# Ten routed groups in one part, scattered in three batches beside the edge lists, with pairs ordered by node tile

## The chip, the cores and the metric

The kernel runs on one core of one Trainium2 chip. The metric is the device time of one execution in microseconds (us). The kernel before took 2046.94, 2055.24 and 2054.68 us in three runs, a median of 2054.68 us. The profiled execution took 2045.04 us, of which 2043.3 us are the span of the trace.

Engines are named as the profile does: PE (matrix multiplications), PEld (its weight loads), ACT (ScalarE), DVE (VectorE), POOL (GpSimd) and SP (SyncE, which here only issues DMAs).

## The reference, cut to what matters

There are 128 graphs of 64 nodes, which make 8192 rows of 256 features. Two layers follow each other; each is a graph step and a feed-forward step, both added to x. The change lies in the feed-forward step of layer 1, except for one piece of memory that it fills in layer 0. That step is:

```python
h = (x_flat @ W_gat).reshape(M, HEADS, NUM_EXPERTS)
e = leaky_relu(a_src[src] + a_dst[dst])         # for every edge, and a loop at every node
alpha = softmax of e over the edges that end in the same node
agg = segment_sum(h[src] * alpha, dst) + b_gat
scores = layernorm(agg).reshape(M, HEADS, NUM_EXPERTS).mean(1)
topk_s, topk_i = top_k(scores, 2)               # 2 of 4 experts for every node
w = softmax(topk_s)
for ei in range(4):
    g = where(topk_i == ei, w, 0).sum(-1)
    out = out + g * (gelu(x @ W1[ei] + b1[ei]) @ W2[ei] + b2[ei])
```

The edges decide by which two experts a node is computed. Until a node's edges are summed, nobody knows which two these are.

## The kernel before

The 8192 rows are 64 node tiles of 128 rows, or 16 groups of 4 tiles. x stays in on-chip memory throughout.

**Layer 0.** Parts of two groups run one after another: a graph step (`graph`), and two parts behind it the first half of the feed-forward step (`gated`), which writes 4 KB rows to the DRAM buffer `hrows`, sorted by expert, with indirect DMAs from POOL (line 775). A row tile is turned by copies of ACT (line 713) into one buffer, `rows`, which must have landed in DRAM before the next group's copies. Beside them DVE looks through chunks of the edge list (`collect`): each chunk is loaded by SP (`src` and `dst`, line 247), searched, and what is left over is stored by SP (`left`, line 284), after which the next chunk uses the same buffer. `hrows` gets zeros at its experts' starts (line 815), from a 128 x 128 tile of zeros.

**Layer 1, two ways to apply the experts.** Groups 0 to 7 (`DENSE`) are computed densely: all four experts for every row (`experts`, `dense`). A unit of this work is one step of the generator `units`: eight for an expert (four of the first matmul with its Gelu, four of the second), 32 for a group, 256 in all. Their results are kept in DRAM (`ystore`) until the gates are known (`kept`, `add`). Groups 8 to 15 are routed: every row is sent only to the buffers of its two experts.

The routed groups come in two parts of 16 tiles. For each part `gates` computes ranks and weights, `route` gives each row its place, `send` copies a row tile twice and scatters it to `zslots` (two indirect DMAs a tile, line 1904), `pairs` takes two tiles of slots at a time through one expert, whose number is read into registers, and stores the result in `yslots`, and `back` gathers two results for every row (line 2100), copies them, and adds them with their weights. Slots of one expert are rounded up to whole pairs of tiles, so a part has RT + 3 = 19 pairs, 38 in all.

**Order of the work in layer 1.** The tables of the graph attention come first; 72 units of dense work lie beside them. A short prologue takes 20 units. Then `edges_of_lists` works through 16 sorted edge lists, one for each group, routed groups first. It has 162 steps; in each of the first 144 POOL gathers 128 edge sources (`got`, line 1585), a copy moves them on three steps later, and a list is summed into `acc` 8 steps behind its last gather. Two of three steps also take a dense unit. From list 6 on each step takes one step of the gates and routes; in the last 18 steps it takes one scatter. The rest of part 0's scatters follow, with units and the gates of the dense groups, then the 38 pairs with part 1's scatters, part 0's gathers and the kept results beside them, then the last 40 units with part 1's gathers beside them.

The order within an engine is drawn up when the program is built: what is ready first goes out, by its place in the text where several are ready. `tc.issue_after(ins)` puts what its block issues on the engine of `ins` behind `ins`. SP and POOL each take their DMAs strictly in order; a DMA that has to wait holds up those behind it.

Of the kernel before, what the change touches and what calls it, by code (L numbers as in the profile page):

```python
# [2 lines left out]

# [64 lines left out]
PARTS = 2  # L68
ROUTED = 4 * PARTS
DENSE = NG - ROUTED  # L70
RT = ROUTED // PARTS * GR
PAIRS = RT + 3
# [8 lines left out]
def kernel(  # L81
# [103 lines left out]
    yrows = dram.tile([NSLOT * P, D], F32, name="yrows")  # L185
    psel = const.tile([P, NT], F32, name="psel")
# [233 lines left out]
    with tc.tile_pool(name="w0", bufs=1, reuse_waits="tile") as w0, tc.tile_pool(name="kp", bufs=1, reuse_waits="tile") as kp:  # L420
# [29 lines left out]
        with tc.tile_pool(name="bg1", bufs=1, reuse_waits="tile") as bg1, tc.tile_pool(  # L450
# [19 lines left out]
            with tc.tile_pool(name="b2", bufs=1, reuse_waits="tile") as b2, tc.tile_pool(  # L470
# [321 lines left out]
                chunks = iter(range(n_chunks))  # L792
                for i in range(n_parts + 2):
# [18 lines left out]
                    if i == 1:  # L812
                        with tc.issue_after(first_made[-1]):
                            for e in range(E0):
                                nc.sync.dma_start(
                                    hrows[e * N : e * N + P, :].rearrange("p (k f) -> p k f", f=P),
                                    none.unsqueeze(1).to_broadcast([P, FD // P, P]),
                                )
# [261 lines left out]
    zns = dram.tile([ROUTED, P, GR * D], F32, name="zns")  # L1080
    zslots = [dram.tile([PAIRS * 2 * P, D], F32, name=f"zslots{h}") for h in range(PARTS)]
    yslots = [dram.tile([PAIRS * 2 * P, D], F32, name=f"yslots{h}") for h in range(PARTS)]
# [485 lines left out]
    def edges_of_lists(pool, psum, td3):  # L1568
# [5 lines left out]
        for step in range(ET * (NB + 2)):  # L1574
            n, at = divmod(step, ET)
            if n < NB:
                b = lists[n]
                if at == 0:
                    fss[n] = pool.tile([P, ET, CH], F32, name="fs")
                    sorting = sort(lists[n + 2], pool, psum) if n + 2 < NB else iter(())  # L1580
                    el = pool.tile([P, ET * P], BF16, name="el")
# [7 lines left out]
                if at == 3:  # L1589
                    to = pool.tile([P, ET, P], BF16, name="to")  # L1590
# [153 lines left out]

    place = [gp.tile([P, 2, RT], I32, name=f"place{h}") for h in range(PARTS)]
    weight = [gp.tile([P, 2, RT], F32, name=f"weight{h}") for h in range(PARTS)]
    pair_e = [gp.tile([P, PAIRS], I32, name=f"pair_e{h}") for h in range(PARTS)]
    T0 = DENSE * GR
    sends = []

    def gates(pool, t0, t1, ranks):
# [3 lines left out]
        def of(name, *shape):  # L1755
            return pool.tile([P, *shape, nt], F32, name=name)
# [4 lines left out]
        def by_node(v, n):  # L1761
# [5 lines left out]
        agg = of("agg", HC)  # L1767
# [4 lines left out]
            sums[:, HEADS:CH, :].rearrange("p (h c) t -> p h c t", c=NEXP),  # L1772
# [55 lines left out]
    def route(h, pool, ranks, psum):  # L1828

        t0 = T0 + h * RT  # L1830
        rk, gt = ranks[t0], gate[:, :, t0 : t0 + RT]
        chosen = pool.tile([P, NEXP, RT], BF16, name="chosen")
        V.tensor_scalar(chosen, rk, 1.5, None, ALU.is_lt)
        flat = chosen.rearrange("p e t -> p (e t)")

        pt = psum()
        nc.tensor.matmul(pt[0 : NEXP * RT, 0:P], flat, ones, start=True, stop=True)
        tots = pool.tile([NEXP * RT, P], BF16, name="tots")
        V.tensor_copy(tots, pt[0 : NEXP * RT, 0:P])
        yield  # L1840
        pr = psum()
        nc.tensor.matmul(pr[:, 0 : NEXP * RT], before, flat, start=True, stop=False)
        nc.tensor.matmul(pr[:, 0 : NEXP * RT], tots, later[:, 0 : NEXP * RT], start=False, stop=True)
        row = pool.tile([P, NEXP, RT], F32, name="row")
        V.tensor_copy(row.rearrange("p e t -> p (e t)"), pr[:, 0 : NEXP * RT])
        pa = psum()
        nc.tensor.matmul(pa[:, 0:NEXP], tots, of_all, start=True, stop=True)
        yield
        full = pool.tile([P, NEXP], I32, name="full")
        V.tensor_scalar(full, pa[:, 0:NEXP], float(2 * P - 1), None, ALU.add)  # L1850
        V.tensor_scalar(full, full, 8, None, ALU.logical_shift_right)
        end = pool.tile([P, NEXP + 1], F32, name="end")
        V.memset(end[:, 0:1], 0.0)
        V.tensor_copy(end[:, 1:], full)
        for e in range(1, NEXP):
# [335 lines left out]
```

## Time and profile before

| | us |
|---|---|
| median of three runs | 2054.68 |
| profiled execution | 2045.04 |
| span of its trace | 2043.3 |
| PE busy | 1877.0 (92%) |
| DVE busy | 1339.2 (66%) |
| ACT busy | 948.5 (46%) |
| POOL busy | 431.2 (21%) |
| first of the 139 gathers that follow the first five | 1392.9 |
| last gather of the edge lists | 1627.8 |
| first matmul of the pairs | 1690.2 |
| first matmul behind the pairs | 1970.7 |
| last matmul | 2039.6 |

The times in the lower half are starts, counted from the start of the span, except the last matmul's, which is its end. Busy times are means over stages with different limits: a stage must be read by itself. An engine's row names what it waited for last. "issue" is time in which it waited for nothing that the trace shows.

### The profile page before, as it was taken

The page shows a single profiled execution, that of the slowest core. Times are in us where ns is not written, and L with a number is a line of the kernel's source. Part 1 is how long each engine was busy: PE and PEld are TensorE (multiplying, and loading weights), DVE is VectorE, ACT ScalarE, POOL GpSimd, SP SyncE. Part 2 cuts the span into 40 slices and gives each one's busy share as a digit, 9 for nine tenths or more (in the row PEclk, how much of TensorE's full clock was granted, in tenths as well). Part 3 has the DMA queues.
Part 4 walks back from the last instruction along what each step waited for, and adds up shares of the span by engine and source line. Part 5 has one row for each costly group of instructions (what it writes and reads, how often), then busy time and mean ns, then how long its engine had stood idle before and what let it go on. Part 6 is the DMA issues. An engine that isn't in the chain of part 4 may idle for free. (4 is left out here: it accounts for less than half of the span.)

```text
span 2043.3 us, 32233 instructions
## 1 busy us (share of the span) xinstructions
PE 1877.0 (92%) x10582; PEld 1329.1 (65%) x10582; DVE 1339.2 (66%) x4364; ACT 948.5 (46%) x1740; POOL 431.2 (21%) x464
## 2 busy tenths in 40 slices
PE   7889989899996999999487999998899999999999
PEld 5444444444455999998354766666666757888876
DVE  6789988861218888887598775857678552334435
ACT  4867677666662222222267677432233333333332
POOL 2011011010110000000442100015566652303223
PEclk9999999989997999999798999999999999999999
DMA  9232223242424444545215211373222248978843
GB/s 296 64 103 102 95 76 127 75 135 69 165 83 165 159 163 151 161 152 154 75 56 157 75 50 54 125 223 77 58 47 66 62 160 275 300 240 279 281 130 98
DMA packets 223037, 274.93 MB, mean 135 GB/s; under 512 B 55696, under 2 KB 175888, under 8 KB 222864
## 3 DMA queue, kind: packets, MB, share of 16 engines
q1 hardware_dynamic: 188976, 212.26, 33.3%
q0 software_dynamic: 23040, 60.22, 9.1%
q8 instruction: 90, 1.47, 0.3%
q10 hardware_dynamic: 10848, 0.30, 0.3%
q14 instruction: 83, 0.68, 0.1%
HBM read 159.40 MB, written 113.22 MB: 133 GB/s over the span
## 5 line engine op out<-in xcount | busy, mean ns | idle before, releaser
L462 PE MATMUL ph<-zT,w 128*128 128x512 f32 x512 | 247.7, 608 | 5.7 <-ACT zT L704 4.7
L973 PE MATMUL py<-wd,hTt 128*128 x1088 | 247.0, 380 | 0.0
L973 PEld LDWEIGHTS py<-wd,hTt 128*128 128x128 f32 x1088 | 202.4, 191 | 24.9
L958 ACT COPY hTt<-th 128x512 f32<-128x512 f32 x136 | 73.2, 589 | 283.3 <-PE th L955 265.9
L1585 POOL DMA_INDIRECT got<-tsrc,esrc x144 | 151.8, 1054 | 179.2 <-DVE esrc L1556 75.6
L1116 PE MATMUL py<-w,hT 128*128 128x256 f32 x736 | 173.6, 388 | 8.0 <-DVE kt L1524 4.6
L1106 PE MATMUL ph<-zT,w 128*128 128x512 f32 x368 | 171.3, 608 | 0.0
L1185 POOL DMA_INDIRECT yin<-yrows,row_y x64 | 65.3, 1021 | 476.4 <-SPq L1029 360.2
L462 PEld LDWEIGHTS ph<-zT,w 128*128 128x128 f32 x512 | 93.2, 194 | 105.4 <-issue 86.2
L1116 PEld LDWEIGHTS py<-w,hT 128*128 128x128 f32 x736 | 138.3, 193 | 34.8 <-issue 10.8
L2070 ACT ACTIVATE hT<-ph,b1e 128x256 f32<-128x256 f32 x152 | 72.1, 474 | 176.2 <-PE ph L2066 100.8
L2066 PE MATMUL ph<-zTp,w1e 128*128 128x256 f32 x608 | 139.0, 382 | 4.3 <-DMA w1e<-in_L_ffn_W_dram 4.3
L1110 ACT ACTIVATE hT<-ph,b 128x512 f32<-128x512 f32 x92 | 63.1, 688 | 163.6 <-PE ph L1106 137.6
L2079 PE MATMUL py<-w,hT 128*128 x608 | 137.5, 379 | 0.0
L2087 DVE TENSOR_TENSOR y<-py,b2e 128x256 f32<-128x256 f32 x76 | 32.2, 424 | 159.8 <-PE py L2079 147.3
L775 POOL DMA_INDIRECT hrows<-rows,pos x64 | 63.5, 992 | 335.3 <-issue 212.5
L2066 PEld LDWEIGHTS ph<-zTp,w1e 128*128 128x128 f32 x608 | 116.5, 192 | 20.6 <-issue 4.5
L624 PE MATMUL pre<-wd 128*128 128x512 f32 x256 | 125.2, 606 | 1.9 <-ACT wd L610 1.3
L465 ACT ACTIVATE hT<-ph,b 128x512 f32<-128x512 f32 x128 | 88.0, 688 | 74.1 <-PE ph L462 71.3
L2079 PEld LDWEIGHTS py<-w,hT 128*128 128x128 f32 x608 | 112.6, 190 | 13.8
L199 DVE TENSOR_TENSOR one<-iota_l,pb 128x2048 bf16<-128x2048 bf16 x96 | 116.7, 1216 | 0.1
L1106 PEld LDWEIGHTS ph<-zT,w 128*128 128x128 f32 x368 | 68.3, 193 | 68.8 <-issue 68.0
(427 smaller groups left out, 3714.6 us busy)
## 6 DMA issues: line engine op xcount, KB each, us to landing
hin<-hrows SPq DMA_DIRECT2D x68, 512.0 KB
w1e<-in_L_ffn_W_dram SPq DMA_DIRECT2D x38, 512.0 KB
yin<-ystore SPq DMA_DIRECT2D x24, 512.0 KB
zslots<-none SPq DMA_DIRECT2D x38, 256.0 KB
zin<-zslots SPq DMA_DIRECT2D x38, 256.0 KB
yslots<-y SPq DMA_DIRECT2D x76, 128.0 KB
ystore<-y SPq DMA_DIRECT2D x72, 128.0 KB
bd<-in_L_ffn_bd_dram SPq DMA_DIRECT2D x68, 128.0 KB
```

What stands on the lines that cost most here:

```text
L199: V.tensor_tensor(o, numbers.unsqueeze(1).to_broadcast(shape), of.rearrange("p (j e) -> p j e", e=2).unsqueeze(2).to_broadcast(shape), ALU ...
L462: nc.tensor.matmul(ph, w1[:, c, q * P : q * P + P], zT[:, c, :], start=(c == 0), stop=(c == 1))
L465: gelus.append(S.activation(hT, ph, AF.Gelu, bias=b1[:, q : q + 1]).ins)
L624: nc.tensor.matmul(pre, xnT[:, c, n * P : n * P + P], wcat[:, c, :], start=(c == 0), stop=(c == 1),)
L958: S.copy(hT[:, i : i + GR, :].rearrange("p q n -> p (q n)"), th)
L973: nc.tensor.matmul(py, hT[:, q, :], wd[:, bass.ds(e, 1), q, :].rearrange("p e f -> p (e f)"), start=(q == 0), stop=(q == NH - 1),)
L1106: nc.tensor.matmul(ph, w1[:, e, c, q * P : q * P + P], zT[:, c, :], start=(c == 0), stop=(c == 1))
L1116: nc.tensor.matmul(py, hTs[q][:, k * P : k * P + P], w2[:, e, q, :], start=(q == 0), stop=(q == NH1 - 1))
L1585: nc.gpsimd.indirect_dma_start(got, None, tsrc, bass.IndirectOffsetOnAxis(ap=esrc[:, b, at : at + 1], axis=0))
L2066: nc.tensor.matmul(ph, w1e[:, c, q * P : q * P + P], zT[:, c, :], start=(c == 0), stop=(c == 1))
L2070: pace[:] = [S, S.activation(hT, ph, AF.Gelu, bias=b1e[:, q : q + 1]).ins]
L2079: nc.tensor.matmul(py, hTs[q][:, k * P : k * P + P], w2[:, e, q, :].rearrange("p e f -> p (e f)"), start=(q == 0), stop=(q == NH1 - 1),)
```

## The change

It does the following.

- Groups 6 to 15 are routed, ten for eight; the dense groups are 0 to 5. All routed groups form one part of 40 tiles, with 43 pairs.
- Each expert has a fixed stretch of `zslots` and `yslots`, long enough for all 5120 rows, so a row's place is known as soon as those before it are counted. A running count (`run`) is carried from tile to tile.
- Gates, routes and scatters come in batches of 4, 3 and 3 groups, all inside the loop over the edge lists; a batch starts when its lists are summed. The scatter reads the loaded row tile itself, without the copy.
- The pairs are put in the order of the node tiles that fill them (`order_pairs`), and their rows' addresses are read into registers. `back` takes a tile when the pairs that may hold its rows are through, so that most gathers lie beside later pairs.
- All 192 dense units lie before the pairs; the gates of the dense groups and the kept results lie beside them.
- The zeros in `zslots` and `yslots` (2 x 20,480 rows of 1 KB) are written in layer 0, as 40 DMAs of 1 MB, five in each of eight parts. They were written to `zslots` alone, 38 DMAs of 256 KB, beside the edge lists.
- Two tiles of the edge lists, `el` and `to`, have one buffer for two.

```diff
-PARTS = 2
-ROUTED = 4 * PARTS
-DENSE = NG - ROUTED
-RT = ROUTED // PARTS * GR
-PAIRS = RT + 3
+ROUTED = (4, 3, 3)
+DENSE = NG - sum(ROUTED)
+STARTS = [DENSE + sum(ROUTED[:h]) for h in range(len(ROUTED))]
+T0 = DENSE * GR
+RT = NT - T0
+CAP = RT * P
+PAIRS = RT + NEXP - 1
...
+    zslots = dram.tile([NEXP * CAP, D], F32, name="zslots")
+    yslots = dram.tile([NEXP * CAP, D], F32, name="yslots")
...
+                zeros = ((to, at) for to in (zslots, yslots) for at in range(0, NEXP * CAP, 8 * P))
                 for i in range(n_parts + 2):
...
+                    if i >= 2:
+                        with tc.issue_after(gelus[-1]) if gelus else ExitStack():
+                            for to, at in islice(zeros, -(-2 * NEXP * CAP // (8 * P * n_parts))):
+                                nc.sync.dma_start(
+                                    to[at : at + 8 * P, :].rearrange("(p r) (k f) -> p (r k) f", r=8, f=P),
+                                    none.unsqueeze(1).to_broadcast([P, 8 * D // P, P]),
                                 )
...
-                    el = pool.tile([P, ET * P], BF16, name="el")
+                    el = single.tile([P, ET * P], BF16, name="el")
...
-                    to = pool.tile([P, ET, P], BF16, name="to")
+                    to = single.tile([P, ET, P], BF16, name="to")
...
     def route(h, pool, ranks, psum):
...
+        for t in range(nt):
+            V.tensor_tensor(run[:, r0 + t + 1, :], run[:, r0 + t, :], chosen[:, :, t], ALU.add)
+            if t % 4 == 3:
+                yield
+        pr = psum()[:, 0 : NEXP * nt].rearrange("p (e t) -> p e t", e=NEXP)
+        nc.tensor.matmul(pr, before, chosen, start=True, stop=False)
+        nc.tensor.matmul(pr, ones, run[:, r0 : r0 + nt, :].rearrange("p t e -> p e t"), start=False, stop=True)
+        row = by_tile("row")
+        V.tensor_tensor(row, pr, bases.unsqueeze(2).to_broadcast([P, NEXP, nt]), ALU.add)
...
+    def order_pairs(pool, psum):
...
+        V.tensor_scalar(own, own, key, None, ALU.is_le)
+        V.tensor_reduce(key, own, AX.X, ALU.add)
+        V.scalar_tensor_tensor(key, key, float(P), own_p, ALU.mult, ALU.add)
+        keys = pool.tile([P, P], F32, name="keys")
+        V.tensor_copy(keys, key.to_broadcast([P, P]))
+        yield
+        pk = psum()[:, 0:P]
+        nc.tensor.transpose(pk, keys, ident)
...
     def send(h, pool):
...
+        for t in range(r0, r0 + 2):
+            load(t)
+        for t in range(r0, r1):
+            if t + 2 < r1:
+                load(t + 2)
             zn = zs.pop(t)
             for j in range(2):
-                z = to["y"]()
-                paced_copy(z, zn)
                 sent = nc.gpsimd.indirect_dma_start(
-                    zslots[h], bass.IndirectOffsetOnAxis(ap=place[h][:, j, t : t + 1], axis=0), z, None
+                    zslots, bass.IndirectOffsetOnAxis(ap=place[:, j, t : t + 1], axis=0), zn, None
                 )
...
-    sz = ctx.enter_context(tc.tile_pool(name="sz", bufs=2, reuse_waits="tile"))
+    sz = ctx.enter_context(tc.tile_pool(name="sz", bufs=4, reuse_waits="tile"))
...
+            for h, n in enumerate(ROUTED):
+                last = STARTS[h] + n - DENSE - 1
+                while taken < ET * (last + 2):
+                    yield
+                yield from gates(ga, STARTS[h] * GR, (STARTS[h] + n) * GR, ranks)
                 yield from route(h, ga, ranks, to["ph"])
-        steps = routes()
-        zeros = ((h, i) for h in range(PARTS) for i in range(PAIRS))
-        for taken, _ in enumerate(edges_of_lists(emp, psm, td3)):
-
-            if taken % 3 == 0:
-                for h, i in zeros:
-                    nc.sync.dma_start(
-                        zslots[h][2 * P * i : 2 * P * i + 2 * P].rearrange("(k p) f -> p k f", p=P),
-                        none.unsqueeze(1).to_broadcast([P, 2, D]),
-                    )
-                    break
-            if taken > ET * (ROUTED // PARTS + 2):
-                next(steps, None)
-
-            if taken >= ET * NB:
-                next(sending)
-            if taken % 3 != 2:
-                next(units)
...
+                ready.append(h)
+            yield from order_pairs(ga, to["ph"])
+
+        def all_sends():
+
+            for h in range(len(ROUTED)):
+                while h not in ready:
+                    yield
+                yield from send(h, sz)
+
+        routing, sending = routes(), all_sends()
+        for taken, _ in enumerate(edges_of_lists(emp, em1, psm, td3)):
+
+            next(routing, None)
+            next(routing, None)
+            next(sending, None)
+            if taken * 5 % 8 < 5:
+                g, n = next(units, (g, n))
...
-            nc.sync.dma_start(z, zslots[h][2 * P * i : 2 * P * i + 2 * P].rearrange("(k p) f -> p k f", p=P))
+            nc.sync.dma_start(z, zslots[rows, :].rearrange("(k p) f -> p k f", p=P))
...
-                nc.sync.dma_start(yslots[h][(2 * i + k) * P : (2 * i + k + 1) * P, :], y)
-                yield h
+                store = nc.sync.dma_start(yslots[rows, :].rearrange("(k p) f -> k p f", p=P)[k], y)
+                alone(store, stores + gathers)
+                stores.append(store.ins)
+                yield m if k else m - 1
...
+    def back():
+
+        later = 4
+        got = {}
         for n in range(2 * RT + later):
             if n < 2 * RT:
                 t, j = divmod(n, 2)
+                while finished < min(t + NEXP - 1, PAIRS - 1):
+                    yield
+                got[n] = backs[n % len(backs)]
+                made = nc.gpsimd.indirect_dma_start(
+                    got[n], None, yslots, bass.IndirectOffsetOnAxis(ap=place[:, j, t : t + 1], axis=0)
                 )
+                gathers.append(made.ins)
             if n >= later:
                 t, j = divmod(n - later, 2)
+                xs = x[:, T0 + t, :]
+                with tc.issue_after(sums[0]):
+                    V.scalar_tensor_tensor(
+                        xs, got.pop(n - later), weight[:, j, t : t + 1], xs, ALU.mult, ALU.add
+                    )
...
+    the_pairs = pairs()
+    next(the_pairs)
+    for g, n in units:
         pass
-    steps = back(PARTS - 1)
-    for n, _ in enumerate(units):
-        next(steps, None)
-        if n % 3 == 2:
+    last_gates, returned, stored = gates(ga, 0, T0, ranks), back(), kept()
+    for n, finished in enumerate(the_pairs):
+        for of in range(2):
+            next(last_gates, None)
+        if n % 3 != 1:
+            next(returned, None)
+        if n > 30 and n % 9 == 8:
             next(stored, None)
```

## The prediction

> **What bounds the kernel now.** I read the table of slices first (PE is at 9 nearly everywhere), then the busy time by stretches of layer 1, then the chain that ended last, POOL's groups of instructions, and last SP's timeline in layer 0, where the change adds DMAs.
>
> Stretches: the edge lists, their last sum, the last scatters, the pairs, the dense tail. Columns are length, then busy time (and count) of PE, PE's weight loads, DVE, ACT and POOL, then clock, DMA share and GB/s.
>
> ```profile
> 1392.00:1628.00 236.00, 224.61 (x1601) 155.56 (x1599) 171.27 (x668) 83.22 (x169) 145.93 (x139) 0.99 0.25 55
> 1628.00:1642.00 14.00, 14.00 (x69) 10.80 (x68) 5.76 (x20) 5.28 (x9) 9.23 (x9) 1.00 0.53 179
> 1642.00:1690.00 48.00, 38.91 (x139) 25.30 (x137) 24.62 (x78) 13.71 (x26) 24.30 (x24) 0.96 0.48 164
> 1690.00:1971.00 281.00, 280.76 (x1366) 246.89 (x1367) 99.01 (x234) 103.90 (x235) 63.51 (x64) 0.99 0.83 261
> 1971.00:2043.00 72.00, 68.58 (x240) 45.20 (x238) 34.45 (x89) 18.43 (x36) 31.56 (x32) 1.00 0.34 104
> ```
>
> PE is busy 95% of the edge stretch and all of the pairs: there, less PE work is less time, as long as nothing else takes its place. The chain around the pairs (start, length, what):
>
> ```profile
> 1678.29 4.04 DMA zslots<-y,place
> 1685.48 4.62 DMA w1e<-in_L_ffn_W_dram
> 1690.24 5.23 PE ph L2066 x16
> ...
> 1959.92 0.44 PE ph L2049 x4
> 1960.36 3.46 PE py L2079 x16
> 1963.81 3.45 PE ph L2066 x16
> ...
> 1984.49 6.87 PE ph L1106 x16
> 1991.36 6.91 PE py L1116 x32
> ```
>
> One pair is 3.45 + 0.44 + 3.46 = 7.35 us, one expert pass of a dense group 6.87 + 6.91 = 13.78 us. POOL in the edge stretch, and two gathers in a row:
>
> ```profile
> L1585 POOL DMA_INDIRECT got<-tsrc,esrc x139 | 146.7, 1055 | 102.4 <-DVE fs L1132 29.8 <-ACT fs L1132 29.3 <-issue 26.3
> L1904 POOL DMA_INDIRECT zslots<-y,place x18 | 19.2, 1064 | 8.9 <-issue 4.5 <-DVE y L1132 2.7 <-DVE y L1120 1.4
> ...
> 1441.40 0.95 POOL L1585 DMA_INDIRECT got<-tsrc,esrc  x1 [0.30 <-ACT fs L1132]
> 1442.65 0.95 POOL L1585 DMA_INDIRECT got<-tsrc,esrc  x1 [0.30 <-issue]
> ```
>
> An indirect DMA holds POOL for 0.95 us at least and is followed by 0.30 us in which nothing is waited for. So the 139 gathers need 146.7 + 139 x 0.30 = 188 us of the 236 us. POOL is hidden, but has only 48 us to spare. Last, the stretch in layer 0 where zeros are written now, and two waits that touch DMA there (total, times, longest):
>
> ```profile
> 33.87 17.25 SPq L815 DMA_DIRECT2D hrows<-none  x8
> 53.97 2.72 SPq L877 DMA_DIRECT2D yrows<-none  x4
> 77.48 0.33 SPq L247 DMA_DIRECT2D src<-in_L_ffn_edge_index_dram  x1
> ...
> 50.00:54.00 4.00, 3.14 (x14) 1.54 (x12) 0.62 (x2) 3.72 (x5) 0.00 (x0) 1.00 0.96 289
> ...
> ACT rows L713 <- DMA hrows<-rows,pos: 17.0, 10, 5.6
> DVE key L251 <- DMA left<-key: 13.7, 8, 2.2
> ```
>
> A fill with 512-byte rows runs at 289 GB/s with the DMA engines full (0.96). The zeros of line 877 go out at 54 us although they are written far behind in the program: a DMA that waits for nothing goes out when SP is free.
>
> **Matmul work.** Two dense groups fewer: 2 x 4 x 13.78 = 110.2 us less. RT grows to 40, so 43 pairs for 38: 5 x 7.35 = 36.7 us more. Net 73.5 us less on PE. Counting units (a group has 32): before, 72 lie in the graph stage, 20 beside the tables, 108 in the edge loop, 16 beside the last scatters, 40 behind the pairs. After, 72, 20 and 100, none later. So the gain comes as 68.9 us behind the pairs, 27.6 us beside the scatters, 13.8 us in the edge loop.
>
> **Edge loop.** It takes in 80 scatters where it had 18, one a step, from about step 62 (the first four lists are summed at step 44, the gates and the route take two steps of their generators a loop step) to step 141. With 100 units instead of 108 a step without a scatter loses 8/162 x 1.72 = 0.08 us of the 1.69 it takes (1392.9 to 1627.8, 139 gathers): 1.61. A step with one takes POOL 1.06 + 0.30 + 0.99 + 0.30 = 2.65 us by mean rows (0.99 is the mean of all 64 scatters), 0.95 + 0.30 + 0.96 + 0.30 = 2.51 by the shortest. PE has 224.6/139 - 0.08 = 1.54 us of work in it. So 59 x 1.61 + 80 x 2.65 = 307 us (296 at the shortest): the last gather moves from 1628 to 1700 (1689). PE draws its units forward and then idles some 60 us.
>
> What queues behind POOL's wait for the first places is the gathers; five buffers cover three steps. The row loads now stand on SP between the ystore stores; a late one stalls POOL, bounded by one landing (4.0 us) for each of three batches: 0 to 12 us. I take 0, since rows are loaded two tiles ahead.
>
> **From the last gather to the first pair.** Before, the last list's sum left PE at 1641.3, 13.5 us behind the last gather. The scatters have landed by then (4.0 us behind step 141), so the 35 us of waiting for them go. What is late next: the list's memory has to come free for the pair buffers, then registers and the weight load, 1684.8 to 1690.2 now, 5.4 us. Bounds: 11 us if these run early, 19 if one after the other. I take 15, the middle, because the trace shows no placement: first pair at 1715, for 1690.2.
>
> **Pairs and end.** 43 x 7.35 + 2 us for the first, slow one (5.23 for 3.45) = 318 us: to 2033. DMA moves 261 GB/s now without holding PE; I count 49.6 MB for the pairs, 10.5 gathered, 8.4 out, 12.6 reloaded, 81 MB in 316 us = 257 GB/s. The same, so no stall. The gathers back wait on each pair's store, but their sums are placed two tiles later, so DVE meets landed data. Behind the last pair nothing covers the way home: y 0.4, store 2.5 (issued 1971.2, the next gather ran at 1973.6), two gathers 2.2, landing 2.2, sum 0.5, out 2.4 = 10.3 us, for 3.7 now: 2043.3. Layer 1 sums to 0, bounds -18 (shortest periods, early loads) to +20 (a stall of 12, late loads).
>
> **Costed at nothing.** Gates of 24 tiles and all 24 reloads now lie beside the pairs, where DVE is busy 99 of 281 us; uncovered, the gates would add about 15 us. Route, order_pairs and the third set of gates add some 15 us to DVE in the edge loop (171 of 236 now). The copies that go (128 of 0.3 to 0.4 us) are off the path. The 38 fills that go lie at 1317 to 1365, with PE 76.7 of 78 us busy: no gain. Single el and to buffers: el is fetched six steps ahead; uncovered, 16 x 2.8 us.
>
> **The new fill in layer 0.** Both buffers now have 20,480 rows: 41.9 MB of zeros, forty 1 MB DMAs with 512-byte rows, 145 us of full DMA engines at 289 GB/s. The order wrapper names a ScalarE instruction and the fill is on SP, so I expect what line 877 shows: it goes out from about 57 us, to about 240 us with the other traffic (some 12 MB). Two things meet it. The scatters of hrows (2.1 MB, four groups in that time) now land as the next copy needs them; if they get half the engines, 2.1 MB at 289 GB/s is 7 us more each: 28 us. The chunk loop of DVE (left out, src in) waits 2 us; behind the 2 MB that SP has queued (7 us: 51 to 58 us at 289 GB/s), seven chunks lose up to 49 us. Ends: 0, all hidden, and 77. I take 20, near the lower end, because PE and DVE have 8 and 12% idle there, and DVE is only 48% and then 21% busy after 400 us, so chunks can slip.
>
> The Trainium skill (DMA: Bandwidth & Descriptors, Queues, rings and completion order) says that each DMA engine goes round its queue rows packet by packet. By that the scatters keep half the engines, the 28 us above; a queue served strictly in order of arrival would cost them only the 7 us of backlog. No row here shows the two queues full together.
>
> **Rivals.** (1) The fill lies in idle DMA time (share 0.3 at 100 to 400 us) and costs 0 for 20 us: 2050, no change. For it: SP's idle gaps. Against: the copy that already waits 5.6 us on hrows. It gets below 2044 only if layer 1 lands more than 6 us under its sum. (2) All forty fills stand in SP's queue ahead of chunk 1's load (77.5 us now): DVE stops until about 205 us, some 100 us lost: 2150. For it, line 877's place; against, SP issued eight fills of 0.5 MB in 17 us, so others can slip between. (3) The edge loop stays PE-bound and the matmul gain arrives: 73.5 less 6.6 of end, 67 us faster: 1990, faster than before. It needs POOL's 188 + 80 x 1.29 = 291 us to fit in 230: scatters of 0.5 us each decide it, and none of 64 took under 0.95. 1.0 us for a scatter with its gap would give 2047.
>
> **How the numbers follow.** 2045.0 (profiled: span 2043.3 and 1.7 around it) + 0 + 20 = 2065; the three runs lie 1.9 to 10.2 us above the profiled one, I add 5: 2070. Forecast 0.47, (1) 0.29, (2) 0.13, (3) 0.07, rest 0.04. The range, 2028 to 2130, leaves out (3), most of (2) and little else; the likeliest case's own is 2050 to 2110. Half a per cent of the median 2054.7, about what a measurement can tell, is 10 us: faster by more (below 2044) takes (3), 0.12 of (1) and 0.05 of the forecast's low end: 0.24; within it lie 0.13 of (1) and 0.07 of the forecast: 0.2; slower: 0.56.
>
> **What would show it.** Right: last gather near 1700 plus the shift of layer 0, POOL periods of 2.5 to 2.65 us where scatters run, PE idle there, first pair 15 us behind, 43 pairs of 7.35 us, 10 us of end. Fills from 57 us at a DMA share near 1, longer waits at lines 713 and 251. Wrong: hidden fills, or scatters that find POOL idle.

## The result and the profile after

The changed kernel took 2126.07, 2125.81, 2132.71 and 2142.27 us, a median of 2129.39 us; the kernel before took 2046.94, 2055.24, 2054.68 and 2049.0 us, a median of 2051.84. The ratio is 1.0391, 95% interval 1.0338 to 1.0444. The forecast was 2070: the direction was right and the size was not. The profiled execution took 2126.07 us (span 2124.3).

Its page, busy tenths in 40 slices of 53 us, shows where: PE falls from 9 to between 5 and 8 from 1487 to 1805 us, while POOL is at 5 to 7 up to 1752 and the granted PE clock at 7 or 8.

```profile
PE   7888889999988999997779999989755578999997
POOL 2011111010110000001521000036667571122222
PEclk9999999999998999998879999999877778999999
```

The stretches of layer 1 after: gathers alone; gathers and scatters; behind the last gather; pairs. Columns as before: length, busy time and count of PE, weight loads, DVE, ACT and POOL, then clock, DMA share, GB/s.

```profile
1385.00:1529.00 144.00, 127.96 (x873) 88.26 (x872) 98.68 (x387) 40.54 (x79) 76.50 (x73) 0.93 0.24 60
1529.00:1768.00 239.00, 143.80 (x798) 91.43 (x798) 93.39 (x411) 48.43 (x92) 155.25 (x154) 0.74 0.29 88
1768.00:1794.00 26.00, 21.74 (x95) 15.89 (x94) 16.18 (x51) 7.70 (x10) 0.70 (x1) 0.97 0.26 73
1794.00:2113.00 319.00, 318.09 (x1544) 279.48 (x1544) 114.10 (x280) 103.23 (x215) 73.74 (x78) 0.99 0.81 254
```

In the second row nobody is the bound: PE is busy 60% of the time, POOL 65% (84% with a gap of 0.30 us behind each of its 154 instructions), DVE 39%. The pairs are full of PE work, as forecast. Cut at the same places, against the profiled execution of before (2043.3):

| part | forecast | after against before |
|---|---|---|
| start to first gather (1365.2, now 1385.1) | +20 | +19.9 |
| first to last gather (262.6, now 382.7) | +72.2 | +120.1 |
| last gather to first pair (62.4, now 26.3) | -47.4 | -36.1 |
| first pair to the end (353.1, now 330.2) | -24.8 | -22.9 |
| sum | +20 | +81.0 |

So 59 of the 61 us that were not foreseen lie between the first gather and the first pair. The waits of that stretch (total, times, longest) name something that the trace of before has for 19 us in all, and this one for 191 us, summed over the engines:

```profile
ACT hT L1121 <- remote: 97.5, 5, 31.0
DVE rows L204 <- remote: 34.1, 3, 21.7
DVE one L1620 <- remote: 29.9, 5, 12.3
DVE acc L1646 <- remote: 20.9, 3, 14.8
DVE y L1131 <- remote: 7.7, 1, 7.7
```

"remote" is a wait that ended on no recorded instruction or DMA. All of these instructions wait for PE. One such place in the timeline of all engines (start, length, what, idle time before and its end):

```profile
1528.49 2.13 PE L1641 MATMUL ps<-r,ol 128*128 128x80 f32 x18
1529.00 1.01 POOL L1943 DMA_INDIRECT zslots<-zn,place  x1 [0.30 <-issue]
1530.32 0.97 POOL L1943 DMA_INDIRECT zslots<-zn,place  x1 [0.30 <-issue]
1530.46 3.64 PE L1117 MATMUL ph<-zT,w 128*128 128x512 f32 x8
...
1548.11 0.98 POOL L1943 DMA_INDIRECT zslots<-zn,place  x1 [0.30 <-issue]
1552.44 0.24 DVE L1646 TENSOR_TENSOR acc<-acc,ps 128x80 f32<-128x80 f32 x1 [14.84 <-remote]
1552.50 0.69 ACT L1121 ACTIVATE hT<-ph,b 128x512 f32<-128x512 f32 x1 [24.71 <-remote]
```

The 18 matmuls that fill `ps` run by 1530.6 and those for `ph` by 1534.1, by the records. DVE's sum of `ps` and ACT's Gelu of `ph` start at 1552.4, some 20 us later, together, and only then can PE reuse `ps`. From 1521.3 to 1549.1 POOL issues indirect DMAs with 0.30 us between them; 3.4 us behind its last, the others go on. The ends of matmuls are modelled in a profile, so these rows alone don't tell whether the matmuls end late or their signals arrive late. The trace also records when PE's semaphore rises (the counter that the other engines wait on), and for this place that settles it: the rises come at 1552.42, 1552.47 and 1552.53 for `ps` and the two `ph`, whose last matmuls end at 1530.6, 1532.4 and 1534.1 in the records. Two `ph` that really ran so late would be 1.7 us apart, not 0.06, so here it is the signals that are late. In the third series below, with the same program, every rise in the edge stage comes within 0.1 us of the recorded end of a matmul that gives a signal; in this run some come up to 22 us behind the last such end.

The fill in layer 0 goes out where the forecast had it. In SP's timeline its first five DMAs are issued at 54 us:

```profile
54.15 14.58 SPq L828 DMA_DIRECT2D zslots<-none  x5
```

A stretch of 50 us in the middle of it (same columns as above) has the DMA engines full:

```profile
150.00:200.00 50.00, 39.53 (x173) 22.43 (x172) 39.29 (x158) 34.14 (x58) 3.83 (x4) 0.94 1.00 305
```

And these are the waits for DMA between 50 and 420 us:

```profile
DVE key L256 <- DMA left<-key: 29.2, 10, 5.7
ACT rows L718 <- DMA hrows<-rows,pos: 12.7, 4, 5.0
```

DVE waits 15.5 us more for `left` than before (13.7), ACT 4.6 us more for `hrows` (8.1; over the whole of the run it is 24.0 for 17.0).

### The profile page after: what moved, and what is told of

Same layout as the page of the kernel before. It is cut to its first block, busy times and chain, and to the rows that moved or that the text cites. A ratio compares the mean times of both kernels' runs of the same rounds, so it can differ in the third digit from the quotient of the medians.

```text
span 2124.3 us, 32111 instructions
## 1 busy us (share of the span) xinstructions
PE 1848.0 (87%) x10380; PEld 1310.0 (62%) x10380; DVE 1320.6 (62%) x4384; ACT 919.8 (43%) x1659; POOL 456.0 (21%) x490
## 5 line engine op out<-in xcount | busy, mean ns | idle before, releaser
L467 PE MATMUL ph<-zT,w 128*128 128x512 f32 x512 | 247.8, 608 | 5.8 <-ACT zT L709 4.8
L2099 ACT ACTIVATE hT<-ph,b1e 128x256 f32<-128x256 f32 x172 | 81.4, 474 | 209.9 <-PE ph L2095 160.3
L2095 PE MATMUL ph<-zTp,w1e 128*128 128x256 f32 x688 | 158.0, 383 | 4.4 <-DMA w1e<-in_L_ffn_W_dram 4.4
L2116 DVE TENSOR_TENSOR y<-py,b2e 128x256 f32<-128x256 f32 x86 | 36.5, 424 | 200.4 <-PE py L2108 166.3
L467 PEld LDWEIGHTS ph<-zT,w 128*128 128x128 f32 x512 | 93.7, 195 | 106.2 <-issue 86.7
L1127 PE MATMUL py<-w,hT 128*128 128x256 f32 x480 | 136.5, 430 | 24.2 <-issue 13.4
L2108 PE MATMUL py<-w,hT 128*128 x688 | 155.6, 379 | 0.0
L2095 PEld LDWEIGHTS ph<-zTp,w1e 128*128 128x128 f32 x688 | 132.4, 193 | 23.0 <-ACT gate L1833 4.6
L2108 PEld LDWEIGHTS py<-w,hT 128*128 128x128 f32 x688 | 127.4, 190 | 15.6
L1117 PE MATMUL ph<-zT,w 128*128 128x512 f32 x240 | 130.6, 677 | 6.4 <-issue 6.4
L1121 ACT ACTIVATE hT<-ph,b 128x512 f32<-128x512 f32 x60 | 41.1, 687 | 216.2 <-remote 97.5
L1127 PEld LDWEIGHTS py<-w,hT 128*128 128x128 f32 x480 | 97.0, 213 | 48.6 <-issue 20.8
L470 ACT ACTIVATE hT<-ph,b 128x512 f32<-128x512 f32 x128 | 88.1, 688 | 72.9 <-PE ph L467 70.3
L2137 POOL DMA_INDIRECT ts<-yslots,place x58 | 54.9, 946 | 214.6 <-DMA yslots<-y 192.6
```

What stands on the lines that cost most here:

```text
L467: nc.tensor.matmul(ph, w1[:, c, q * P : q * P + P], zT[:, c, :], start=(c == 0), stop=(c == 1))
L470: gelus.append(S.activation(hT, ph, AF.Gelu, bias=b1[:, q : q + 1]).ins)
L1117: nc.tensor.matmul(ph, w1[:, e, c, q * P : q * P + P], zT[:, c, :], start=(c == 0), stop=(c == 1))
L1127: nc.tensor.matmul(py, hTs[q][:, k * P : k * P + P], w2[:, e, q, :], start=(q == 0), stop=(q == NH1 - 1))
L2095: nc.tensor.matmul(ph, w1e[:, c, q * P : q * P + P], zT[:, c, :], start=(c == 0), stop=(c == 1))
L2099: pace[:] = [S, S.activation(hT, ph, AF.Gelu, bias=b1e[:, q : q + 1]).ins]
```

## Experiments

Theories. A: indirect DMAs that POOL issues one right after the other make PE's results be seen late. B: SP, in order, waits 78.1 us for scatters to land before it may load the next row tile, and the stores and lists behind it are late. C: the 10.5 MB that the scatters write do it. D: runs of scatters stand ahead of gathers in POOL's order. E: POOL being busy is enough. F: a loop of waits; POOL waits 76 us for copies to free its five buffers, and these wait for PE. The edits are shown shortened. Where one time is given, the kernel ran once; seven runs of the kernel before spread over 8.9 us in the third series and 6.3 us in the fourth, four of the changed kernel over 16.5 us in the result above, so smaller differences in time say nothing.

The runs were made in five series, on several chips, and the series differ. Where the kernel before takes 2046 to 2061 us, every kernel shows such waits; where it takes 2018, none has any. Results are therefore set beside the kernel before of the same series. The changed kernel itself ran only for the result above and in the third series, so where the first, fourth or fifth series is compared with its 2129 us, this is across series. Whether the chip or its condition decides was not settled: the second and the fourth series, one of each kind, carry the same chip number. "Late" below is the sum of these waits over all engines in the edge stage.

### First series (before 2048.52)

**Gathers for scatters.**

```diff
-    zslots, bass.IndirectOffsetOnAxis(ap=place[:, j, t : t + 1], axis=0), zn, None
+    backs[len(sends) % 7], None, zslots, bass.IndirectOffsetOnAxis(ap=place[:, j, t : t + 1], axis=0)
```

> Each of the 80 scatters of the edge loop is replaced by an indirect gather of the same size (128 rows of 1 KB, zslots to a spare slice in SBUF), so that POOL issues as many indirect DMAs of the same cost, but nothing is written to zslots: the routed rows are left out of the computation. zn buffers come free without waiting for a scatter. Theory A (indirect DMAs issued back to back by POOL hold up the signals with which PE tells that a matmul is done): the waits of DVE and ACT that end on no recorded instruction stay above 60 us, first pair near 1794 (within 15), time 2110 to 2135. Theory B (SP waits in order for scatters to land before it can load the next row tile, and the stores and list loads behind it are late): SP's 78 us of waits for scatters are gone, so the first pair comes near 1735 and the time is near 2070. Theory C (the 1 KB rows written to DRAM do it): near 2070 too.

2149.01 us, first pair at 1817.8, late 152 us. Its waits:

```profile
DVE one L1620 <- remote: 56.6, 6, 18.8
ACT hT L1121 <- remote: 39.2, 5, 24.8
DVE found L1555 <- remote: 21.5, 2, 20.4
```

SP waits 3.6 us for row tiles instead of 78 and nothing is written to `zslots`, yet the loop is longer. B and C fall. A holds, though its upper bound of 2135 was too low.

**Plain writes of SP for scatters.**

```diff
-    sent = nc.gpsimd.indirect_dma_start(zslots, ..., zn, None)
+    r = (j * RT + t) * P
+    sent = nc.sync.dma_start(zslots[r : r + P, :], zn)
```

> Each scatter is replaced by a plain DMA of SP that writes the same 128 rows of 1 KB to fixed rows of zslots (the order by expert is left out of the computation). POOL issues the gathers only. Theory A: the waits that end on no recorded instruction are gone, the loop is as long as PE's work (222 us from 1413), first pair 1650 to 1670, time 1985 to 2005. Theory B: SP still waits in order, now for the loads and writes of rows, and holds up stores and lists: most of the 59 us stay, time above 2030. Theory C: the same 10.5 MB are written, so the stalls stay, above 2030.

2032.73 us, first pair at 1702.2, 92 us earlier than with scatters, late 41 us. The same bytes are written, so C falls again. A has the direction, not the size: the gathers alone leave 41 us, and the time is above A's window.

**One gather, one scatter in turn.**

```diff
+    with tc.issue_after(sends[-1]) if sends else ExitStack():   # each gather
+    with tc.issue_after(last_got[-1]):                           # each scatter
```

> The order on POOL is bound: each gather behind the last scatter that was written before it and each scatter behind the last gather, so that one gather and one scatter take turns and eight scatters in a row no longer stand ahead of a gather. Nothing else changes. Theory A: POOL still issues back to back, the waits that end on no recorded instruction stay, 2105 to 2135. Theory D (the runs of scatters keep the gathers from DVE and ACT, and these, in order, starve PE): the step takes POOL's 2.65 us, first pair near 1735, time near 2070.

2143.44 us, first pair at 1811.0, late 148 us. D falls: the order hardly matters.

**Eleven buffers for row tiles.**

```diff
-    zs[t] = pool.tile([P, D], F32, name="zn")          # 4 buffers
+    zs[t] = kept_zn[t % 11]                            # these and 7 slices of dead tables
```

> Eleven buffers instead of four for the row tiles that are scattered (the seven others are slices of tables that are not read any more). Nothing else changes. Theory A: SP's waits for scatters fall from 78 us to under 15, but the waits that end on no recorded instruction stay above 60 us and the time within 15 us of 2126. Theory B: with SP free the stores and lists are on time, first pair near 1735, time near 2070.

2128.53 us, first pair at 1797.3, late 139 us. SP's waits for scatters, which were 78.1 us:

```profile
SPq L1938 <- DMA zslots<-ts,place: 27.2, 8, 6.5
SPq L1938 <- DMA zslots<-zn,place: 7.0, 5, 3.4
SPq L1938 <- DMA zslots<-td,place: 4.6, 2, 2.7
```

They are halved (A's 15 was too hopeful) and the time does not move. B falls a second time.

### Second series (before 2017.63)

**Half rows**, and **POOL copies for scatters**:

```diff
-    zslots, bass.IndirectOffsetOnAxis(...), zn, None
+    zslots.rearrange("n (h f) -> (n h) f", h=2), bass.IndirectOffsetOnAxis(...), zn[:, 0:P], None
```

```diff
-    sent = nc.gpsimd.indirect_dma_start(zslots, ..., zn, None)
+    for i in range(2):
+        sent = nc.gpsimd.tensor_copy(backs[(2 * len(sends) + i) % 7], zn)
```

> The scatters write 512 bytes of each row instead of 1 KB, to 40960 half rows (half of the routed rows' content is left out). As many indirect DMAs, half the bytes. Theory A (indirect DMAs issued back to back hold up PE's signals): waits that end on no recorded instruction above 60 us, time 2110 to 2150. Theory C' (the bytes moved by these DMAs do it): half of the 59 us go, about 2095.

> Each scatter is replaced by two copies of the same row tile on POOL, inside SBUF (the routed rows are left out). POOL stays busy for about as long, but issues no DMA for it. Theory A: the waits that end on no recorded instruction shrink to what the run with plain writes of SP had (40 us) or less, and the time is 2000 to 2040. Theory E (POOL being busy is enough, by whatever it holds of SBUF): the waits stay above 60 us and the time above 2100.

2067.58 and 2028.6 us, late 0 in both. As no kernel of this series has late results, neither tells the theories apart here; the question of bytes stays with the first two runs.

**24 buffers for gathered edges**, and **the fill moved to layer 1's graph stage**:

```diff
-    ahead = ctx.enter_context(tc.tile_pool(name="ahead", bufs=5, reuse_waits="tile"))
+    ahead = ctx.enter_context(tc.tile_pool(name="ahead", bufs=24, reuse_waits="tile"))
```

```diff
     behind[:] = [nc.sync.dma_start(ystore[g, k, :, e * D : e * D + D], y).ins]
+    for rows, at in islice(zeros, 2):
+        with tc.issue_after(behind[0]):
+            nc.sync.dma_start(rows[at : at + 8 * P, :]..., none[0]...)
```

> 24 buffers instead of five for the gathered edge rows. Theory F (a loop of waits: five buffers make POOL wait 76 us for copies of ScalarE and VectorE, which wait for the late signals): without it POOL issues its 224 DMAs in some 300 us, first pair near 1715, time near 2050. Theory A alone: POOL issues more densely, the signals are held up as much or more, first pair between 1760 and 1810, time 2095 to 2140.

> The forty fills of 1 MB stand behind the first twenty stores of layer 1's graph stage, two each, instead of the chunks of layer 0. Nothing else changes. If the 20 us at the start of the edge stage are the fill's price in layer 0: the first gathers of the edge lists run near 1365 instead of 1385, and the time is about 2106. If the fill costs as much wherever it stands, or if the 20 us are not its price, 1385 and 2126. What happens in the edge loop stays as it is in either case.

2044.26 and 2056.1 us, first pairs at 1712.9 and 1723.8, no late results in either; with the fill moved the first gathers run at 1362.9. What the two are worth needs the changed kernel in a series without late results, which is the next one.

### Third series (before 2018.97)

> The changed kernel again, on the chip of this series, since the chips differ: on one the kernel before takes 2048 us and runs of the changed kernel show waits that end on no recorded instruction, on another it takes 2018 us and no run of variants shows them. If the late signals belong to the chip and not to the kernel alone: on a chip where before takes about 2018, after has none of these waits, its first pair lies near 1744 (the 1724 of the late fill and 20), and after takes 2070 to 2080; on a chip where before takes about 2048, after is again at 2120 to 2135. If they belong to the kernel: they are there on every chip, and after is 75 to 85 us above before.

> The kernel before, for its trace on the chip of this series. If the 31 us between the chips are late signals of PE: the stretches where POOL issues gathers one after the other (tables, edge lists, gathers back in layer 1's graph stage) are the ones that are longer on the slower chip, and the pairs, where POOL issues one every 3.7 us, take 7.35 us on both.

The changed kernel takes 2068.54 us here, a ratio of 1.0251 (1.0228 to 1.0274), with no late results at all. The kernel before takes 2019.87 us. Up to 964 us the two traces of before agree within 0.1 us; the 25 us between them arise in the two stretches where POOL gathers without pause: 6 us beside the gathers of layer 0's results (64 of them take 180.4 us in the first profile, 174.2 here), and 19 us in the edge lists (262.6 against 243.5). The stretch of gathers and scatters of the changed kernel, here:

```profile
1505.00:1708.00 203.00, 134.96 (x800) 90.87 (x798) 95.15 (x408) 50.10 (x92) 155.82 (x153) 0.80 0.35 104
```

and the edge lists of the kernel before:

```profile
1358.00:1602.00 244.00, 239.29 (x1695) 168.74 (x1694) 182.10 (x697) 85.80 (x170) 157.17 (x153) 0.99 0.29 67
```

In the first POOL is the bound: 155.8 us of work and 153 gaps of 0.30 us are 201.7 of 203. In the second PE is, with 239.3 of 244. That is the mechanism that was forecast; the first pair follows at 1734.8.

> 24 buffers for gathered edge rows again, beside the changed kernel on the same chip. Theory F: 25 to 35 us less than the changed kernel where signals are on time (POOL no longer waits for copies and issues without a pause until its last DMA); where signals are late, POOL is still without a pause, and the gain is at least as large, 30 to 80 us. Theory A alone: no gain where signals are late.

> 24 buffers for the gathered edge rows and the fill beside layer 1's graph stage, both together. If the two gains add: 45 to 55 us less than the changed kernel, which is within 1% of the kernel before. If the late fill takes DMA time from the tables or the gathers, less than the sum.

24 buffers: 2047.63 us, 21 less than the changed kernel (25 to 35 were expected); POOL issues without pause to its last DMA and the first pair is at 1716.5 instead of 1734.8. F holds where results are on time. Both edits: 2032.02 us, ratio 1.0062 (1.0038 to 1.0086). That is 36.5 us less than the changed kernel, not 45 to 55: the fill moved away saves 15 us at the first gathers when alone (1378.0 to 1362.9), but here they start at 1368.1. This is the fastest version of the change that was found, and it is still slower than the kernel before.

### Fourth series (before 2046.48)

**The fill beside layer 0's second matmul stage, with 24 buffers**, and **nine routed groups with 12 buffers**:

```diff
     stored = nc.sync.dma_start(yrows[t * P : t * P + P, :], y).ins
+    for to, at in islice(zeros, 1):
+        with tc.issue_after(stored):
+            nc.sync.dma_start(to[at : at + 8 * P, :]..., zero...)
```

```diff
-ROUTED = (4, 3, 3)
+ROUTED = (4, 3, 2)
-            if taken * 5 % 8 < 5:
+            if taken * 4 % 5 < 4:
```

> 24 buffers for the gathered edge rows, and the forty fills beside layer 0's second matmul stage (one behind each of the first forty stores of yrows, 629 to 964 us), where PE is busy 94% of the time and the DMA engines 47%. Theory F and a hidden fill: where signals are on time the first gathers are 20 us earlier than in the changed kernel, the loop is bound by POOL, and the time is 2015 to 2030, within 0.6% of before. If the fill delays the loads of that stage: above 2030. Where signals are late (before near 2048): theory F 2050 to 2075, theory A alone above 2090.

> As g1, but with 12 buffers, and nine groups routed in batches of four, three and two instead of ten; the dense units left for the edge loop go from 100 to 132, four in five steps. POOL issues 8 scatters less (10 us), there are four pairs less (29 us), and PE has 55 us more in the loop, where it idles 70 us in the run with 24 buffers. If PE takes them up: 25 to 39 us less than g1, 1980 to 2000 where signals are on time, and faster than before. If the loop becomes PE's: the loop is longer and the gain is 0 to 15 us.

> POOL copies for scatters again (the routed rows are left out). On a chip with late signals, theory A: waits that end on no recorded instruction at most 40 us, time 2030 to 2060; theory E (POOL being busy is enough): above 60 us and above 2100. On a chip without: 2020 to 2035, as before, and nothing is told apart.

2206.8 us (ratio 1.0788, 1.0746 to 1.083) and 2166.06 us (1.058, 1.056 to 1.06). Two things went wrong. The fill costs far more there: the first gathers run at 1430.9, 46 us later than in the changed kernel, and the last load of `hin`, at the end of that stage, goes out at 1023.5 instead of 978.4. And with results late, 24 buffers do not help: from first gather to first pair it takes 439 us (409 with five buffers), late 206. POOL copies: 2077.26 us, late 28. So E falls: POOL is busy and PE's results are nearly on time. A's window of 2030 to 2060 was missed: the loop takes 325.1 us instead of the 296.7 of the second series, some 28 us more, which is about what is late. Nine groups with 12 buffers are 41 us below ten with 24, but two things were changed at once and the loop is full of late results (147 us), so what nine groups are worth stays open.

### Fifth series (before 2061.22)

**Pauses between the DMAs** (h2 has two copies a scatter), and 24 buffers alone.

```diff
     sends.append(sent.ins)
+    with tc.issue_after(sent.ins):
+        nc.gpsimd.tensor_copy(backs[len(sends) % 7], zn)
```

> One copy on POOL (some 0.45 us, of no use) behind each of the 80 scatters, so that POOL issues an indirect DMA every 1.5 us instead of every 1.27 us where it does not wait; nothing else changes and POOL has 36 us more to do. Theory A (the density of the indirect DMAs makes PE's signals late), on a chip with late signals (before near 2048): the waits that end on no recorded instruction fall from the 192 us of the changed kernel to below 120, and the time from 2126 to 2085 to 2115, although POOL does more. If density is not the cause: 2126 to 2165. On a chip without late signals (before near 2018): 2070 to 2100, nothing is told apart.

> Two such copies behind each scatter: a DMA every 1.7 us, which is what the edge lists of the kernel before have (1.69). Theory A on a chip with late signals: waits that end on no recorded instruction below 70 us, time 2070 to 2105. If density is not the cause: 2126 to 2200. On a chip without late signals: 2080 to 2120.

> 24 buffers for gathered edge rows, nothing else. Theory A on a chip with late signals: POOL issues more densely, so the waits that end on no recorded instruction are at least the changed kernel's 192 us, and the time is 2120 to 2170. Theory F (POOL's own waits for copies are what the loop loses): 2050 to 2100. On a chip without late signals: 2040 to 2050 as before.

Late results: 57 us with one copy, 9 us with two, 250 us with 24 buffers. The waits of the run with two copies have one such line:

```profile
DVE one L1620 <- remote: 9.3, 4, 4.3
```

Its groups of POOL instructions between 1500 and 1790 us show that POOL is now the bound (222 us of busy time in these three rows, 18 in a fourth, and 52 us of idle time, most of it the 0.30 us gaps):

```profile
L1596 POOL DMA_INDIRECT got<-tsrc,esrc x89 | 97.4, 1095 | 29.5 <-ACT fs L1143 12.4 <-issue 11.0 <-DVE fs L1143 1.9
L1945 POOL DMA_INDIRECT zslots<-zn,place x78 | 78.3, 1004 | 22.8 <-issue 22.2 <-DVE table L1917 0.3 <-DMA zslots<-zn,place 0.3
L1952 POOL COPY ts<-zn 128x256 f32<-128x256 f32 x112 | 46.3, 439 | 0.2
```

The first two of the run with 24 buffers:

```profile
ACT hT L1121 <- remote: 114.2, 6, 35.2
DVE acc L1646 <- remote: 42.0, 2, 22.0
```

The same 224 DMAs, set 1.27, 1.5 or 1.7 us apart on average where POOL need not wait: the waits go from 191 to 57 to 9 us, and to 250 when POOL never has to pause for a buffer. In these series the density decides, which is A. It is not the mean over the whole stage: from the first gather to the first pair that lies between 1.7 and 1.8 us in the kernel before, the changed kernel and the three runs here. What differs is how long POOL goes on in that stage without a pause: at most 12 us in the kernel before, 45 in the changed kernel, 17 and 15 with one and two copies, 38 with 24 buffers. How long it may go on without harm was not measured. The times are 2124.85, 2153.16 and 2167.77 us: with one pause the loop is as long as the changed kernel's (381.1 us from first to last gather, 382.7), though POOL has more to do, and with two it is longer (405.9). Against the kernels before of their own series one pause is 64 us more, two are 92, the changed kernel 78, so pauses bring nothing that single runs can show. Both time windows for the pauses were missed. F falls here: 24 buffers are 107 us above the kernel before of this series, where the changed kernel is 78 above that of its own, and they gain 21 us where results are on time.

What stays open is why the series differ, by what path POOL's DMAs reach PE's signals, and why PE itself runs slowly in such a stretch (last section).

## Why the prediction was right or wrong

**Matmul work and pairs: right.** 100 units and 43 pairs; the pairs take 318.1 us (318 forecast), and the chain of after

```profile
1804.12 3.45 PE ph L2095 x16
1807.57 0.44 PE ph L2078 x4
1811.46 3.45 PE ph L2095 x16
```

shows the same 7.35 us a pair as before. DMA moves 254 GB/s beside them (257 forecast) and holds nobody up. The end is 12.1 us behind the last matmul (10.3 forecast; the terms as printed add up to 10.2).

**Edge loop: this step failed.** It said that 59 steps of 1.61 us and 80 of 2.65 bring the last gather from 1628 to 1700, 334.8 us behind the first. In the third series, where results are on time, it took 330.3 us, with POOL as the bound: the mechanism and the size were right. In the run that the forecast was for it took 382.7. The step counted what POOL needs and what PE needs, and held them independent: that PE's results would be seen late had no term in the sum, and they were, with 191 us of waits. The trace of before had nine waits of 26.9 us on "remote" in all, 18.8 of them in the edge stage, where gathers come every 1.69 us on average:

```profile
ACT hT L1110 <- remote: 9.2, 1, 9.2
DVE one L1609 <- remote: 6.4, 2, 3.4
DVE acc L1635 <- remote: 2.9, 1, 2.9
```

They were not read as a price that grows when POOL's pauses go.

**"PE draws its units forward": wrong in every series.** From last gather to first pair 15 us were taken (11 to 19); it is 26.3 us, and 26.5 in the third series. The order on PE is fixed when the program is built, so its idling lies inside the loop, and 21.7 of the last 26 us are still dense units and list sums; the weights of the first pair are loaded only behind them (4.0 us). With the edge loop's 47.9 us too few, these 11.3 make up the 59.

**Layer 0: the sum was right, its parts less so.** Fills went out from 54 to 248 us, at a DMA share of 0.99 to 1.00 from 100 us on. By the last half of layer 0 the shift is 14.5 us (`hin` loads from 643.6 instead of 629.1), which is the fill's price, and 12.7 at the last table load. The rest arises between that and the first gather (33.9 us instead of 26.7). There DVE has a wait that the forecast did not have:

```profile
DVE td L1975 <- DMA tdst<-td: 7.2, 1, 7.2
```

It subtracts in `td` ahead of the first gathers, and a store of `td` has to be through first; before, that work began at 1381.7, behind the first gather. So that the sum comes to 19.9 is partly luck. With the fill moved, first gathers come 15.1 us earlier. Rivals (1), hidden fills, and (2), DVE stopped until 205 us, did not happen.

**The rule that was weighed.** By the Trainium skill (DMA: Bandwidth & Descriptors, Queues, rings and completion order), scatters beside the fill get half of each engine's turns, which gave the estimate of 28 us. ACT waited 4.6 us more for `hrows`; the larger part was the chunk loop of DVE, 15.5 us, which that rule did not price. The measurement decides: the estimate was several times too high here. Its weak point was the half: while the four scatters of a group and the fill moved together (128.7 to 136.4, 170.8 to 177.8 and 212.9 to 219.8 us), the scatters had 74 to 81% of the engines' time and took 6.9 to 7.7 us, for 5.7 to 7.0 before. A packet of a scatter has 3.6 KB on average here and one of the fill 0.5 KB, so equal turns would not be equal time; whether the engines really took turns by packets was not measured.

**Rival (3)**, the loop bound by PE, needed scatters of 0.5 us. With no scatters on POOL at all the time was 2032.73, not 1990, so even free scatters would not have brought the whole matmul gain in that series.

In the series without late results the changed kernel takes 2068.54 us, but that the forecast's 2070 lies so near is chance: it was worked out from a profile with 27 us of late results in it. Against the kernel before of the same series it is 49.6 us more, where 15 were forecast. Cut into the same parts, the profiled executions of the third series differ by +19.9, +86.8, -35.9 and -23.9 us, +46.9 in all. The loop bound by POOL is as long as forecast, but the loop bound by PE that it replaces is 19 us shorter there than in the profile the forecast was made from.

## What to carry to other kernels

An engine that is off the critical path can cost more than its own time: before you fill the pauses of an engine that issues indirect DMAs, look in the trace of before for waits that end on nothing, and at how far apart its DMAs stand there and how long they go on without a pause. Work that moves off PE is worth nothing where POOL then sets the pace, and PE, whose order is fixed, will not catch up behind it by itself. Set every run beside the kernel before of the same series, and take a trace of both there: 34 of the 81 us were not the same in another series.

## What the hardware showed that was not expected

- Indirect DMAs of POOL with 0.30 us between them leave other engines waiting up to 35 us at a time for PE's results in some series, and in none of the eight traces of two others, with the same program (the changed kernel: 191 us of waits, and 0). The direction of the DMA and SP's part in it mattered little (152 us of waits with gathers only, 139 with SP's waits halved).
- PE itself slowed down in one such stretch, in which no signal of PE is recorded from 1560.6 to 1576.3. In the timeline of after, each matmul of a sum of 18, which runs in 0.12 us elsewhere (2.13 us for 18), stands by itself, with nothing to wait for and at first at full clock:

```profile
1566.36 0.23 PE L1641 MATMUL ps<-r,ol 128*128 128x80 f32 x1 [0.81 <-issue]
1567.09 0.23 PE L1641 MATMUL ps<-r,ol 128*128 128x80 f32 x1 [0.50 <-issue]
1567.81 0.32 PE L1641 MATMUL ps<-r,ol 128*128 128x80 f32 x1 [0.49 <-issue]
1569.89 0.36 PE L1641 MATMUL ps<-r,ol 128*128 128x80 f32 x2 [1.75 <-issue]
1572.02 0.29 PE L1641 MATMUL ps<-r,ol 128*128 128x80 f32 x1 [1.77 <-issue]
```

- An idle PE lost its clock and got it back late. PE stopped at 1534.1; the stretches of 2 us of after show the granted clock going to 0.5 some 2 us later and back to 1.0 only some 4 us after PE started again at 1552.7:

```profile
1534.00:1536.00 2.00, 0.10 (x1) 0.00 (x0) 0.00 (x0) 0.00 (x0) 1.57 (x2) 1.00 0.70 249
1536.00:1538.00 2.00, 0.00 (x0) 0.00 (x0) 0.70 (x3) 0.00 (x0) 1.39 (x3) 0.55 0.39 121
1554.00:1556.00 2.00, 2.00 (x4) 0.67 (x2) 1.86 (x5) 0.07 (x1) 1.70 (x2) 0.50 0.07 5
1558.00:1560.00 2.00, 1.68 (x4) 0.38 (x2) 2.00 (x11) 1.79 (x3) 1.61 (x2) 1.00 0.25 71
```

  So a wait can cost more than its length. The mean matmul of a dense unit's first half went from 608 to 677 ns; but in the third series it went from 599 to 642 without a late result, so much of this belongs to PE's idling behind POOL.
